# A graph network on one core: the fifth recurrent step computed with tokens on the partitions

## The chip, the cores and the metric

The kernel runs on one core of one Trainium2 chip. The metric is the device time of one execution in microseconds (us); three executions are shown by their median. A profiled execution adds a trace: every instruction with its engine, start, length and tiles. The engines are TensorE (PE: matrix products and transposes), VectorE (DVE), ScalarE (ACT), GpSimd (POOL) and SyncE (SP, which here issues nearly all transfers).

## The reference

128 graphs of 64 nodes, 256 features per node, in f32. Four layers follow each other, each as `x = x + layer(relu(layernorm(x)))`: two attention layers with the graph's adjacency (8 heads), five steps of a gated recurrent unit over the graph, and a gated graph convolution. The recurrent layer is what changes:

```
def _gru_cell(m, h, w_ih, w_hh, b_ih, b_hh):
    gi = m @ w_ih.T + b_ih
    gh = h @ w_hh.T + b_hh
    i_r, i_z, i_n = jnp.split(gi, 3, axis=-1)
    h_r, h_z, h_n = jnp.split(gh, 3, axis=-1)
    r = jax.nn.sigmoid(i_r + h_r)
    z = jax.nn.sigmoid(i_z + h_z)
    n = jnp.tanh(i_n + r * h_n)
    return (1.0 - z) * n + z * h
A = (adj != 0).astype(x.dtype)
h = x
for l in range(weight.shape[0]):            # 5 steps
    m = jnp.einsum('bnd,de->bne', h, weight[l])
    agg = jnp.einsum('bij,bid->bjd', A, m)
    h = _gru_cell(agg, h, w_ih, w_hh, b_ih, b_hh)
return h * mask[..., None]
```

## The kernel before

Two graphs make a pair (128 tokens, one per partition), four pairs a group of 512 tokens, and 16 groups make the input. A group passes through `front` (both attention layers), `entry` (the norm ahead of the recurrence), five steps of `gru`, and `back` (the last layer), while its neighbours are in other stages.

**The recurrent step.** `h` stands with features on the partitions: 128 partitions, two blocks of features, 512 tokens in two halves of 256. The step's matrix `weight[l]` is multiplied into `w_ih` beforehand (`fuse_weights`), so a step sums neighbours first (`agg`, small 64*64 tiles) and then needs the products of `h` with `w_hh` and of `agg` with the fused `gv`. Each 2x2 block product is done by Strassen's seven products in Winograd's form instead of eight: `product(i)`, i = 1 to 7, on blocks of `h` and `agg` and on differences of blocks (`Th`, made by POOL, and `Ta`, made by DVE). In each product the 128x128 weight block is the stationary operand and 256 tokens move, once for each of three gates and both inputs: 42 matmuls of 256 columns. They accumulate in four PSUM banks (`gb`, `gc` for the gates r and z, `nb`, `nc` for n), which all groups share through four slots of the tag `g`, taken in order. ACT copies partial sums out (`saved`), DVE adds a bank and a copy (`summed`), and `update` computes the gates: tanh on ACT, products on DVE, one subtraction on POOL. After steps one to four `turned` transposes the new `h` on TensorE (`hT`), because the next neighbour sum wants tokens on the partitions. The last group's fifth step is done by halves of tokens (`by_halves`, `update_half`), so that its first half can go on early.

**The last layer.** `back_half` turns the final `h` back to tokens on the partitions by eight TensorE transposes a group (`hx`, line 1375), adds it to `x` under the node mask (line 1382), takes the norm, and makes three products by seven (`l3b`, `l3c`; 384 columns) or, at the end, plainly (`f`, `gate`). `adjT`, the transposed adjacency of a group scaled by its degree, comes from `blk` (`adjblk`), which POOL fills from the adjacency tile in `front`.

**What sets the order.** Nothing runs in the order of the source. `Plan` collects every operation with a cost, an engine and a key (a due time in units of a group, set by `strand(base, span)` around the stage), and then picks for each engine, in time by its own costs, the ready operation that is due first. Banks and buffers are slots that it hands out. `CHANGE`, `BESIDE`, `ALONE` and `TURNING` are its costs and preferences for changes of TensorE's tile form (`WIDE`, 64*64, 64*32, transposes); `FRONT`, `BACK`, `STEP`, `LOCK`, `ENTRY`, `FIRST`, `FUSE` and their kin place the stages. The result is one fixed order of instructions for each engine.

Names in the trace: `gv`, `gates` fused weights and their copy in HBM; `qw`, `kept` the same for attention; `s`, `o` scores and weighted values of attention; `e` the exponentials; `xn`, `lnT`, `hT` the norm and its transposes; `cp` copies (`p1g`, `ug` and so on); `sg`, `sn` gates.

## Time and profile before

| | before |
|---|---|
| median of 3 executions | 2500.83 us (2500.80 to 2502.65) |
| the profiled execution, its own time | 2501.22 us |
| its span, first to last instruction | 2499.3 us |
| granted TensorE clock | 0.998 |
| DMA issues: fused weights `gv` | 80 of 1344 KB, 5.9 us to landing |
| DMA issues: `qw` | 203 of 192 KB, 2.4 us to landing |

The span is what the trace covers; the profiled time has 1.9 us around it. A busy share is an average over all stages, so the views in the prediction also take one stage alone. In a line of the timeline stand start and length in us, engine, source line, operation, output and inputs, sizes and count. In a line of the groups: busy us, mean ns of one, and what ended the idle time before it. In a line of the waits: total us, times, longest.

### The profile page before, as it was taken

How to read it: one execution, taken by the hardware profiler on the slowest of the kernel's cores; microseconds unless marked ns; L12 is line 12 of the kernel's file. 1: busy time of each engine (PE TensorE's matmuls, PEld its weight loads, DVE VectorE, ACT ScalarE, POOL GpSimd, SP SyncE). 2: the span in 40 equal slices, each digit the busy share in tenths (PEclk: the TensorE clock that was granted, in tenths of full speed). 3: DMA queues.
4: the chain of work that ended last, by engine and by line, in shares of the span. 5: the costliest groups of instructions: out<-in, count | busy, mean ns of one | idle time of the engine just before them, and what ended most of it. 6: DMA issues, size and time to landing. Idle time of an engine off the chain costs nothing.

```text
span 2499.3 us, 58765 instructions
## 1 busy us (share of the span) xinstructions
PE 2476.8 (99%) x24057; PEld 2130.1 (85%) x24057; DVE 1880.6 (75%) x4396; ACT 1308.5 (52%) x2654; POOL 895.9 (36%) x894
## 2 busy tenths in 40 slices
PE   9999999999999999999999999999999999999997
PEld 7788888888888888888888888888888888888885
DVE  6667777777777777787778777787777777877776
ACT  3455554555555455555555555555454555645544
POOL 5633433334233342433434233343333424332221
PEclk9999999999999999999999999999999999999999
DMA  6422212112222121212113122122211212211110
GB/s 211 158 71 86 72 54 98 65 53 84 72 80 72 61 75 66 100 52 80 59 63 102 50 97 74 53 80 72 80 68 60 76 66 80 68 50 71 52 69 19
DMA packets 78267, 188.60 MB, mean 75 GB/s; under 512 B 14803, under 2 KB 66853, under 8 KB 67109
## 3 DMA queue, kind: packets, MB, share of 16 engines
q1 hardware_dynamic: 77872, 184.71, 21.7%
q8 instruction: 192, 3.15, 0.5%
q14 instruction: 87, 0.70, 0.1%
q10 hardware_dynamic: 116, 0.04, 0.0%
HBM read 166.70 MB, written 18.02 MB: 74 GB/s over the span
## 4 chain that ended last, share of the span: by engine, by line
PE 97%; DVE 1%; ACT 0%; issue 0%; DMA 0%; POOL 0%; DVEq 0%; ACTq 0%
PE gb L994 22%; PE gc L994 17%; PE nb L994 11%; PE nc L994 8%; PE qkvb L711 6%; PE qkvc L711 5%; PE y L879 4%; PE agg L1034 3%; PE l3b L1339 3%; PE s L775 3%; PE l3c L1339 2%; PE hT L547 2%; PE lnT L547 2%; PE o L843 2%; PE o L851 1%; PE gv L930 1%
## 5 line engine op out<-in xcount | busy, mean ns | idle before, releaser
L1103 POOL TENSOR_TENSOR sn<-h,sn 128x512 f32<-128x512 f32 x158 | 202.9, 1287 | 544.5 <-ACT sn L1101 544.5
L533 POOL TENSOR_TENSOR rstd<-pw,few 128x2 f32<-128x2 f32 x128 | 96.3, 755 | 490.1 <-DVE pw L532 445.2
L994 PE MATMUL gb<-Th,w_hh 128*128 128x256 f32 x960 | 249.3, 382 | 0.0
L994 PE MATMUL gb<-Ta,gv 128*128 128x256 f32 x960 | 246.8, 380 | 0.0
L963 POOL TENSOR_TENSOR Th<-h 128x256 f32<-128x256 f32 x160 | 121.2, 778 | 299.8 <-PE nb L994 196.3
L799 POOL TENSOR_TENSOR e<-e,mask 128x512 f32<-128x512 f32 x128 | 177.5, 1406 | 111.5 <-ACT e L797 111.4
L994 PEld LDWEIGHTS gb<-Ta,gv 128*128 128x128 f32 x960 | 177.6, 190 | 22.1 <-issue 0.2
L994 PEld LDWEIGHTS gb<-Th,w_hh 128*128 128x128 f32 x960 | 175.6, 190 | 23.9 <-issue 2.4
L1101 ACT ACTIVATE sn<-sn,b_n 128x512 f32<-128x512 f32 x158 | 113.9, 722 | 143.8 <-DVE sn L1099 143.8
L1105 DVE SCALAR_TENSOR_TENSOR sn<-sg,sn 128x512 f32<-128x512 f32 x158 | 120.5, 769 | 74.4 <-POOL sn L1103 74.2
L994 PE MATMUL gc<-h,w_hh 128*128 128x256 f32 x640 | 167.7, 384 | 0.1
L994 PE MATMUL gc<-agg,gv 128*128 128x256 f32 x640 | 164.3, 379 | 0.0
L1086 ACT ACTIVATE sg<-sg,b_rz 128x512 f32<-128x512 f32 x158 | 106.5, 714 | 81.2 <-DVE sg L1066 81.2
L963 POOL TENSOR_TENSOR Th<-h,Th 128x256 f32<-128x256 f32 x160 | 144.8, 905 | 8.4 <-DVE h L1107 2.8
L552 ACT ACTIVATE hT<-lnT 128x512 f32<-128x512 f32 x96 | 57.1, 594 | 166.9 <-PE lnT L547 166.8
L994 PE MATMUL nb<-Ta,gv 128*128 128x256 f32 x480 | 144.0, 382 | 0.0
L994 PE MATMUL nb<-Th,w_hh 128*128 128x256 f32 x480 | 143.1, 380 | 0.0
L1097 DVE SCALAR_TENSOR_TENSOR sn<-sg,sn 128x512 f32<-128x512 f32 x158 | 117.7, 752 | 32.8 <-ACT sn L1208 28.3
L994 PEld LDWEIGHTS gc<-h,w_hh 128*128 128x128 f32 x640 | 116.2, 190 | 26.6 <-ACT sn L1208 4.0
L1099 DVE SCALAR_TENSOR_TENSOR sn<-sn 128x512 f32<-128x512 f32 x158 | 136.6, 871 | 2.4
L1047 DVE TENSOR_TENSOR Ta<-agg 128x256 f32<-128x256 f32 x160 | 100.2, 643 | 50.5 <-PE nb L994 27.7
L994 PEld LDWEIGHTS gc<-agg,gv 128*128 128x128 f32 x640 | 121.3, 190 | 16.7 <-issue 0.2
(228 smaller groups left out, 6559.4 us busy)
## 6 DMA issues: line engine op xcount, KB each, us to landing
gv<-gates SPq DMA_DIRECT2D x80, 1344.0 KB, 5.9
qw<-kept SPq DMA_DIRECT2D x203, 192.0 KB, 2.4
x<-in_x_dram SPq DMA_DIRECT2D x32, 256.0 KB, 2.9
out_dram<-x SPq DMA_DIRECT2D x32, 256.0 KB, 2.5
gates<-gv SPq DMA_DIRECT2D x5, 1344.0 KB, 5.7
adjq<-in_adj_dram SPq DMA_DIRECT2D x8, 256.0 KB, 4.7
gw<-in_L_gnn_weight_dram SPq DMA_DIRECT2D x5, 256.0 KB, 6.2
kept<-s SPq DMA_DIRECT2D x8, 128.0 KB, 1.9
```

The source lines that it names most:

```text
L711: nc.tensor.matmul(bk[:, j * P : (j + 1) * P], lhs, rhs, start=first and j == 0, stop=True, skip_group_check=True)
L799: pool(1225, lambda e=e: nc.gpsimd.tensor_tensor(e.tile, e.tile, bias_at(pp)[:, None, :].to_broadcast([P, 4, 2 * NODES]), op=ALU.mult), [e ...
L963: pool(690, lambda: nc.gpsimd.tensor_tensor(T[:, i, :], x(), y(), op=ALU.subtract), reads, [(T, i)])
L994: nc.tensor.matmul(bank_[:, col * HALF : (col + 1) * HALF], at(g, n), rhs(), start=first and j == 0, stop=True, skip_group_check=True)
L1047: vec2(dve(256), lambda: nc.vector.tensor_tensor(Ta[:, i, :], x(), y(), op=ALU.subtract), reads, [(Ta, i)])
L1086: sca(act(TOK, 1.5), lambda k=k, col=col: nc.scalar.activation(g_v[:, :, k, :], g_v[:, :, k, :], AF.Tanh, bias=b_rz[:, col : col + 1], sca ...
L1097: vec2(dve(TOK), lambda: nc.vector.scalar_tensor_tensor(a_(), r(), 1.0, a_(), op0=ALU.add, op1=ALU.mult), [*ts[0], n_v], [n_v])
L1099: vec2(dve(TOK), lambda: nc.vector.scalar_tensor_tensor(a_(), a_(), 0.5, b_(), op0=ALU.mult, op1=ALU.add), [n_v], [n_v])
L1101: sca(act(TOK, 1.5), lambda: nc.scalar.activation(a_(), a_(), AF.Tanh, bias=b_n[:, oc : oc + 1]), [n_v, b_n], [n_v])
L1103: pool(1230, lambda: nc.gpsimd.tensor_tensor(b_(), hh(), a_(), op=ALU.subtract), [*hp, n_v], [n_v])
L1105: vec2(dve(TOK), lambda: nc.vector.scalar_tensor_tensor(b_(), z(), 1.0, b_(), op0=ALU.add, op1=ALU.mult), [*ts[1], n_v], [n_v])
L1339: pe(mm(384), lambda: nc.tensor.matmul(bk[:, : 3 * P], b(), w3[:, :, n, :], start=first, stop=True, skip_group_check=True), [w3, *reads], ...
```

## The change

In the fifth step the operands change places: a block of 128 tokens of `h`, `agg` or their differences is the stationary operand, and the weights of all three gates move, 384 columns at once. The result has tokens on the partitions, so that the step works on `ht` (the transposed `h` that the neighbour sum used) and leaves its result there; `back_half` reads it, and `hx` goes. A bank now holds one half-block of 128 tokens with four parts: the n gate's input side, r, z, and the n gate's hidden side; `fuse_weights` stores the last step's gates in the order n, r, z for that. Biases lie along the free dimension, so they can no longer ride on ACT as a scalar per partition: they are rows (`b_row`, loaded by six DMAs and summed once by POOL), which POOL adds to each saved copy. The block of product 4, which has no saved copy to add, leaves its banks by four ACT copies (`taken`), and DVE adds the bias rows. The gates' tanh becomes one ACT instruction over 1024 elements. `adjT` is made in `back`, from a `blk` that two SP DMAs of 64 KB per group fill from HBM in place of POOL's copies. Buffer counts follow (`h` 4 to 3, `ht` 2 to 3, `adjT` 4 to 2), and the planner gets other costs and due times.

```diff
-CHANGE = ((0, 95, 95, 0), (190, 0, 170, 140), (150, 135, 30, 100), (0, 95, 95, 0))
-BESIDE = 0.45
-ALONE = 0.15
-TURNING = 0.25
+CHANGE = ((0, 95, 95, 0), (290, 0, 170, 190), (250, 135, 30, 150), (0, 95, 95, 0))
+BESIDE = 0.52
+ALONE = 0.17
+TURNING = 0.46
...
-FRONT_LAST = 0.05
-FRONT_SPAN = 0.95
-BACK = -0.1
-BACK_LAST = 0.3
+FRONT_LAST = 0.17
+FRONT_SPAN = 1.03
+BACK = 0.0
+BACK_LAST = 0.43
...
-STEP = 0.0
-STEP_LAST = -0.1
-STEP_SPAN = 0.5
-LOCK = 0.35
-BACK_END = 0.15
-ENTRY = -0.05
-FIRST = -1.2
-FIRST_SPAN = 1.0
+STEP = -0.08
+STEP_LAST = -0.07
+STEP_SPAN = 0.4
+LOCK = 0.23
+BACK_END = 0.18
+ENTRY = 0.63
+FIRST = -1.31
+FIRST_SPAN = 1.02
...
-FUSE = -1.1
-FUSE_SPAN = 0.2
+FUSE = -1.22
+FUSE_SPAN = 0.33
...
+        b_row = new("b_row", [P, 2, 4, P], 1)
...
+        dma(768, load_b, [], [b_row, more], 6)
+        pool(1225, lambda: nc.gpsimd.tensor_tensor(
+            b_row[:, :, 1:3, :], b_row[:, :, 1:3, :], more.tile, op=ALU.add), [b_row, more], [b_row])
...
+            if by_token:
+                tokens.send(ht)
+                final[g] = ht
+                yield
+                continue
...
+    def last_step(nm, h, Th, Ta, agg, gv, banks, operand, by_both, whole, halves):
+        def product(i, which, of_h, first=False):
+            n = WEIGHTS[i]
+            b, reads = operand(i, h, Th, by_both) if of_h else operand(i, agg, Ta, whole)
+            w = w_hh if of_h else gv
+            for t in range(2):
+                bk = banks[which][t]
+                pe(mm(384), lambda t=t, bk=bk: nc.tensor.matmul(
+                    bk[:, P:] if of_h else bk[:, : 3 * P], b()[:, t * P : (t + 1) * P], w[:, :, n, :],
+                    start=first, stop=True, skip_group_check=True), [w, reads], [bk])
...
+        def saved(which, n, oc):
+            out = []
+            for t in range(2):
+                c = new("cp", [P, 4, P], 5, f"{n}{t}_{nm}")
+                bk = banks[which][t]
+                sca(act(512), lambda c=c, bk=bk: nc.scalar.activation(
+                    c.tile, bk.tile.rearrange("p (g f) -> p g f", g=4), AF.Copy), [bk], [c])
+                pool(1225, lambda c=c: nc.gpsimd.tensor_tensor(c.tile, c.tile, b_row[:, oc], op=ALU.add),
+                     [c, b_row], [c])
+                out.append(c)
+            return out
...
+        def summed(oc, half, which, others):
+            sg, sn = s[half if halves else oc]
+            for t in range(2):
+                bk, p = banks[which][t], 2 * t + oc if halves else 2 * half + t
+                o, o_at = others[t], lambda o=others[t]: o.tile
+                for dst, key, part in ((sg, "g", lambda x: x[:, 1:3, :]), (sn, "n", lambda x: x[:, 0:4:3, :])):
+                    vec(dve(256), lambda dst=dst, part=part, bk=bk, p=p, o_at=o_at: nc.vector.tensor_tensor(
+                        dst[:, p], part(bk.tile.rearrange("p (g f) -> p g f", g=4)), part(o_at()), op=ALU.add),
+                        [bk, o], [(dst, p)])
...
+        def taken(oc, half, which):
+            ps = slice(oc, PAIRS, 2) if halves else slice(2 * half, 2 * half + 2)
+            for t in range(2):
+                bk, p = banks[which][t], 2 * t + oc if halves else 2 * half + t
+                for dst, part in zip(s[half if halves else oc], (slice(1, 3), slice(0, 4, 3))):
+                    sca(act(256), lambda dst=dst, part=part, bk=bk, p=p: nc.scalar.activation(
+                        dst[:, p], bk.tile.rearrange("p (g f) -> p g f", g=4)[:, part, :], AF.Copy), [bk], [(dst, p)])
+            for dst, part in zip(s[half if halves else oc], (slice(1, 3), slice(0, 4, 3))):
+                vec2(dve(512), lambda dst=dst, part=part: nc.vector.tensor_tensor(
...
+        summed(0, 0, 1, saved(0, "p1", 0))
...
+        both(5, 1, True)
+        p5 = saved(1, "p5", 1)
+        both(6, 0)
+        u = saved(0, "u", 0)
+        both(3, 1)
+        summed(0, 1, 1, u)
+        update(0)
+        both(7, 0)
+        summed(1, 1, 0, p5)
+        both(4, 0)
+        taken(1, 0, 0)
+        update(1)
+        yield
...
-        for gp in range(2):
-            s = slice(gp * NODES, (gp + 1) * NODES)
-            pool(350, lambda s=s: nc.gpsimd.tensor_copy(blk[s, :, s], adjq[s, sel, :]), [adjq], [(blk, gp)])
...
+        def fill():
+            for gp in range(2):
+                s = slice(gp * NODES, (gp + 1) * NODES)
+                nc.sync.dma_start(blk[s, :, s], adj_t[s, g * PAIRS : (g + 1) * PAIRS, :])
+
+        dma(128, fill, [], [blk], 2)
...
-        pe(437, turn, [(h, (0, half)), (h, (1, half)), ident], [ps], mode=TURN)
...
-                xt[:, p, :], ps[:, i * D : (i + 1) * D], cols[:, 18 + t : 19 + t], xt[:, p, :],
+                xt[:, p, :], h_by_token[:, p, :], cols[:, 18 + t : 19 + t], xt[:, p, :],
```

Removed with it are `by_halves` and `update_half`; the last group's fifth step takes another order of the same new products (6, 7, 4, then 5 and 3), by halves of tokens.

## Prediction

> **What bounds the kernel now.** I read the page's first and fourth parts, then busy time by stage, then TensorE's waits, then its timeline.

> ```profile
> span 2499.3 us, 58765 instructions
> PE 2476.8 (99%) x24057; PEld 2130.1 (85%) x24057; DVE 1880.6 (75%) x4396; ACT 1308.5 (52%) x2654; POOL 895.9 (36%) x894
> PE 97%; DVE 1%; ACT 0%; issue 0%; DMA 0%; POOL 0%; DVEq 0%; ACTq 0%
> ```
> ```profile
> 1177.78:1329.89 152.11, 152.11 (x1504) 131.81 (x1503) 117.45 (x277) 81.59 (x167) 54.69 (x54) 1.00 0.22 73
> ```
> ```profile
> PE f L1310 <- ACT hT L552: 2.2, 2, 1.1
> ...
> PE hx L1375 <- DVE h L1141: 1.4, 1, 1.4
> ```

> The chain that ended last is 97% TensorE. The second fence is one period (one group of four pairs) from the middle: length, then busy time of PE, weight loads, DVE, ACT, POOL. TensorE has no gap in it at all, at full clock. All its listed waits add up to about 10 us, in the first 130 us and the last 40. So time changes by what is issued on TensorE, unless another engine comes so late that gaps open.

> A matmul's listed duration is modelled and overlaps the next, so I price by start to start:

> ```profile
> 1205.30 1.03 PE L994 MATMUL gb<-Th,w_hh 128*128 128x256 f32 x4
> 1206.16 0.60 PE L547 MATMUL hT<-ident,h 128*128 128x128 f32 x4
> 1206.60 0.60 PE L994 MATMUL nb<-h,w_hh 128*128 128x256 f32 x2
> ...
> 1209.19 0.59 PE L994 MATMUL nb<-Ta,gv 128*128 128x256 f32 x2
> 1209.72 1.10 PE L775 MATMUL s<-kexp,qk 64*64 64x128 f32 x32
> 1210.64 1.11 PE L1034 MATMUL agg<-A,ht 64*64 64x64 f32 x64
> 1211.68 0.66 PE L1280 MATMUL adjT<-ident,adjblk 128*128 128x128 f32 x4
> 1212.18 1.03 PE L994 MATMUL gb<-h,w_hh 128*128 128x256 f32 x4
> ```
> ```profile
> 123.86 1.10 PE L775 MATMUL s<-kexp,qk 64*64 64x128 f32 x32
> 124.90 1.13 PE L994 MATMUL gb<-Th,w_hh 128*128 128x256 f32 x4
> 125.86 0.61 PE L711 MATMUL qkvb<-hT,qw 128*128 128x128 f32 x4
> ```
> ```profile
> 2441.82 0.81 PE L1339 MATMUL l3c<-w,hTT 128*128 128x384 f32 x2
> 2442.47 0.81 PE L1339 MATMUL l3b<-w,hTT 128*128 128x384 f32 x2
> ```

> Each f32 matmul is two records. 1205.30 to 1206.16: four records of 256 columns take 0.86, so 0.216 each. 1206.16 to 1206.60: a transpose takes 0.109. 2441.82 to 2442.47: 384 columns take about 0.323 each. Small-tile work (s, o, agg: 64*64 or 64*32) costs at its edges. Entering: two records before s take 0.53 instead of 0.43, so 0.10. Ending: s takes 1.04 before a wide matmul (123.86 to 124.90) but 0.92 before agg of the same tile, so 0.12. After it: the first wide matmul costs 0.10 more (0.96 for four), a transpose only 0.06 more (0.50 for four).

> [...] L1099, from SBUF alone, averages 871 ns where POOL works beside it, and its twin L1132 689 ns in the tail, where POOL is nearly idle.

> **The change, part by part.**

> 1. *The turn back goes.* The fifth step leaves h by token, so hx (L1375) disappears:

> ```profile
> L1375 PE MATMUL hx<-ident,h 128*128 128x128 f32 x128 | 19.2, 274 | 1.4 <-DVE h L1141 1.4
> ```
> 128 x 0.109 = **-14.0 us**, all on the saturated engine.

> 2. *The fifth step's products.* Per group 42 matmuls of 256 columns become 28 of 384: the same 10,752 columns. 1344 records x 0.216 = 290.3 become 896 x 0.3225 = 289.0 to 289.4: **-0.9 us**. Weight loads fall by a third and stay hidden.

> 3. *Other durations in the plan.* They reorder only. I counted both built orders on PE. Of 208 small blocks (agg, s, o), those that follow one of the same tile go from 24 to 39; runs of small blocks from 138 to 152; runs left to a wide matmul from 118 to 93, to a transpose from 20 to 59. So +14 x 0.10 - 25 x 0.10 + 39 x 0.06 - 15 x 0.12 = **-0.6 us**.

> 4. *Other engines.* Durations from:

> ```profile
> L730 DVE TENSOR_TENSOR qk<-qkvc,qu 128x256 f32<-128x256 f32 x58 | 24.4, 420 | 32.5 <-PE qkvc L711 30.4 <-ACT qu L726 0.6
> L1103 POOL TENSOR_TENSOR sn<-h,sn 128x512 f32<-128x512 f32 x158 | 202.9, 1287 | 544.5 <-ACT sn L1101 544.5
> L1058 ACT ACTIVATE p1g<-gb 128x512 f32<-128x512 f32 x80 | 47.7, 597 | 45.0 <-PE gb L994 44.9
> ```
> DVE: three pairs of sums (686 + 743 ns) become 12 sums of 420 and two bias adds of about 685: 4.3 to 6.4, +2.1 us a group, 34 in all: 77% of the new span. POOL: 96 bias adds x 1.29 = 124, less 19 for the block copies (L1265): 40%. ACT: about 0.7 less a group, since two gates share one tanh of 1024 (an estimate of 1.03 us, from 597 at 512 and 376 at 256, L724). None comes near 99%, so I cost these at **nothing in the middle**; the cover is TensorE's other work. That cover is what the rivals test.

> 5. *Moved to SP.* 32 fills of adjblk (64 KB) and six bias loads join 411 DMAs. A fill waits only for the adjT transposes of a group one period earlier; behind it stand gate-weight loads (5.9 us to land), needed a step later. The bias loads stand behind the kept stores; behind them stand the second gates store and w3. The bias rows are first needed in step five of group 0, over 200 us later. POOL's one extra add is 1.3 us there. Nothing on the path; bounds 0 to +3 for the start.

> 6. *The tail.* Here other engines set the end. From product 4's end to the last group's first lnT, TensorE had 12.5 us of work and the chain took 14.2 (2456.9 to 2471.12). The new order leaves 11.4 us. The new chain is four copies 1.5, two adds 1.4, tanh 1.0 and 0.6, five DVE steps 3.4, x 0.85, norm 2.5: 11.3, and over a dozen handovers and sums of the other half squeezed in, some 14 again. So it is about 2.6 late instead of 1.7: **+0.9**; bounds -2 (the hx wait of 1.4 goes and nothing replaces it) to +5 (the b_row adds queue behind the other half on DVE).

> Sum: -14.0 - 0.9 - 0.6 + 0.9 = **-14.6 us** against the profiled 2501.2 (span 2499.3 and 1.9 around it), so 2486.6. The median shown, 2500.8, is 0.4 lower: 2486.2, rounded to **2486**. Without parts 5 and 6, a period should fall from 152.0 to about 151.0.

> **Rivals.** A change under 0.2%, 5.0 us, is about what a measurement of this kernel cannot tell from none.

> *A, likeliest (0.70):* as summed; own range 2481 to 2491.

> *B, gaps close too (0.11):* of 10 us of waits at start and end up to half go, since the reordered start and the turnless tail suit the engines. 2476 to 2481. For it: hx itself waited 1.4. Against: f after hT (2.2) is the same code.

> *C, start and last groups open gaps (0.12):* the spread-out weight fusion, or the DVE-bound last chain at its upper bound, costs 5 to 15: 2491 to 2501, about half of it still faster. For it: these are the only places with waits now.

> *D, slower (0.07):* DVE becomes late inside every fifth step. Product 5 restarts bank gc only when product 2 has been summed out; in the new order 1.96 us of other PE work stands between, the two sums of a bank need 0.84, and p1 must already have gone ACT 0.6, POOL 1.29. In the list, the bias adds share POOL with mask products (1.4 each) and the next Th. If the sums come 2.1 us late, the gain of 0.98 a period is gone; 3.5 us late adds 1.4 x 16 = 22: 2508. [...] Against: product 1's copies stand 9 us ahead of product 5, and in the old order the same bank had 1.74 us for one sum of 0.69 and no wait shows.

> That the plan's new durations do not help is counted in part 3; were they worth nothing, 2486.8.

> **How the numbers follow.** A and B are faster; of C about half lies below 2495.8, the rest within 0.2%; D is slower. Faster 0.87, same 0.06, slower 0.07. Range 2478 to 2496: it leaves out D, B's lower half and C's end.

> **What would show it.** Right: hx gone; 896 records of 384 columns at 0.323 in the step; a middle period of 151.0 with PE busy throughout; PE waits in all still near 10 us. Wrong: a wait of gc or nc on DVE in every period (D), a period above 151.5, or waits before 130 us and after 2400 us that exceed 15 us (C).

## The result, and the profile after

| | median (us) | lowest to highest | ratio to the kernel before, 95% interval |
|---|---|---|---|
| changed kernel | 2510.56 (8 runs) | 2507.73 to 2512.51 | 1.0033 [1.0024, 1.0042] |
| before, beside it | 2502.66 (8 runs) | 2500.80 to 2503.07 | |
| changed kernel, a second session | 2505.95 (14 runs) | 2502.09 to 2509.91 | 1.0016 [1.0008, 1.0024] |
| before, beside it | 2501.19 (32 runs) | 2500.43 to 2503.16 | |

The change made the kernel slower, by 4.8 to 7.9 us, where a gain of some 15 was forecast. The changed kernel also spreads more: 8 us between its own runs where the kernel before has 3. The spread, and the part of the loss that falls in the middle, have one cause, found below (experiments 1 to 5); the start and the tail lose time of their own.

The page of the kernel after, its first and fourth parts:

```profile
span 2508.4 us, 58053 instructions
PE 2475.2 (99%) x23481; PEld 2027.1 (81%) x23481; DVE 1928.9 (77%) x4524; ACT 1290.7 (51%) x2634; POOL 992.0 (40%) x959
```
```profile
PE 90%; DVE 8%; issue 1%; ACT 1%; POOL 0%; DMA 0%; DVEq 0%; ACTq 0%
```

DVE has its forecast 77%, POOL its 40%: the busy shares were right and gave no warning. The chain tells more: TensorE fell from 97% of it to 90%, DVE rose from 1% to 8%.

Two periods of the middle (from one group's `adjT` transposes to the next), busy time by stage of the kernel after: length, then PE, weight loads, DVE, ACT, POOL.

```profile
711.09:862.28 151.19, 151.19 (x1473) 125.12 (x1466) 118.98 (x285) 80.41 (x166) 60.38 (x58) 1.00 0.22 73
1014.34:1166.38 152.04, 151.63 (x1472) 125.02 (x1466) 120.42 (x285) 80.41 (x166) 59.80 (x58) 1.00 0.22 73
```

The work and its order are the same in both. One is 151.2 long without a gap, near the 151.0 forecast; the other is 152.0, and TensorE has lost 0.4 us to idle and more to records that start late. The forecast period exists, but not always.

TensorE's waits of the kernel after (total us, times, longest):

```profile
PE hom L1482 <- DVE F L1402: 5.4, 1, 5.4
PE qkvb L726 <- DVE v L747: 4.6, 11, 1.5
PE y L894 <- issue: 1.6, 1, 1.6
...
PE hT L562 <- DVE h L1130: 1.3, 2, 1.0
```

`hx` is gone from the list. New are one wait of 5.4 us in the tail and one on DVE's line 747 that comes back eleven times, nine of them in the middle (2.8 us together).

**An account of the span.** I took the interval from each TensorE record's start to the next and subtracted the median of such intervals (same kind, columns and neighbours) in the trace of before. The sum of these prices is the issue sum; what is above it is the excess: gaps and records at a lower rate. The start is the first 450 us, the tail the last 95 us before TensorE's last record. The span adds 1.35 us ahead of the first record and 11 to 13 after the last.

| kernel | issue sum | excess, start | middle | tail | span of the profiled run |
|---|---|---|---|---|---|
| before | 2466.1 | 8.0 | 3.5 | 7.7 | 2499.3 |
| changed | 2450.5 | 16.0 | 14.9 | 14.2 | 2508.4 |
| changed, second session | 2450.5 | 17.2 | 10.8 | 13.8 | 2504.9 |
| no_bias | 2450.5 | 14.4 | 4.9 | 13.9 | 2496.7 |
| new_plan | 2466.7 | 12.0 | 4.6 | 12.2 | 2509.3 |
| old_plan | 2461.5 | 10.9 | 20.6 | 20.3 | 2526.1 |
| swap | 2450.5 | 14.5 | 6.9 | 14.6 | 2499.4 |
| swap_mm | 2455.7 | 14.8 | 6.3 | 8.1 | 2497.7 |

The forecast saving of issue came in full: 2466.1 - 2450.5 = 15.6. It was eaten by 8.0 us more excess in the start, 11.4 in the middle and 6.5 in the tail; the stretch after the last record gave 1.3 back. Sum +9.0; the spans differ by 9.1.

### The profile page after: what moved, and what is told of

Same layout as the page of the kernel before. It is cut to its first block, busy times and chain, and to the rows that moved or that the text cites. A ratio compares the mean times of both kernels' runs of the same rounds, so it can differ in the third digit from the quotient of the medians.

```text
span 2508.4 us, 58053 instructions
## 1 busy us (share of the span) xinstructions
PE 2475.2 (99%) x23481; PEld 2027.1 (81%) x23481; DVE 1928.9 (77%) x4524; ACT 1290.7 (51%) x2634; POOL 992.0 (40%) x959
## 4 chain that ended last, share of the span: by engine, by line
PE 90%; DVE 8%; issue 1%; ACT 1%; POOL 0%; DMA 0%; DVEq 0%; ACTq 0%
PE gb L1012 17%; PE gc L1012 13%; PE nb L1012 9%; PE nc L1012 6%; PE qkvb L726 5%; PE y L894 5%; PE qkvc L726 4%; PE agg L1057 3%; PE l3b L1424 3%; PE gb L1194 3%; PE nb L1194 3%; PE s L790 2%; PE lnT L562 2%; PE l3c L1424 2%; PE hT L562 2%; PE o L858 2%
## 5 line engine op out<-in xcount | busy, mean ns | idle before, releaser
L1126 POOL TENSOR_TENSOR sn<-h,sn 128x512 f32<-128x512 f32 x128 | 165.0, 1289 | 670.6 <-ACT sn L1124 670.5
L1012 PE MATMUL gb<-Th,w_hh 128*128 128x256 f32 x768 | 197.6, 380 | 0.9 <-DVE sg L1089 0.9
L1012 PE MATMUL gb<-Ta,gv 128*128 128x256 f32 x768 | 197.3, 379 | 0.0
L1012 PEld LDWEIGHTS gb<-Ta,gv 128*128 128x128 f32 x768 | 141.5, 190 | 19.8
L894 PE MATMUL y<-w_L_gnn_Wo,oT 128*128 128x256 f32 x512 | 142.8, 383 | 2.0 <-issue 1.6
L1128 DVE SCALAR_TENSOR_TENSOR sn<-sg,sn 128x512 f32<-128x512 f32 x128 | 105.9, 827 | 48.3 <-POOL sn L1126 48.3
L726 PEld LDWEIGHTS qkvb<-hTQ,qw 128*128 128x128 f32 x696 | 101.5, 191 | 31.3 <-DVE v L747 11.4
L894 PEld LDWEIGHTS y<-w_L_gnn_Wo,oT 128*128 128x128 f32 x512 | 95.3, 190 | 30.0 <-issue 4.4
L803 POOL TENSOR_TENSOR x<-x,r_L_gnn_bo 128x512 f32<-128x512 f32 x64 | 83.1, 1299 | 85.7 <-DVE xn L592 74.6
L726 PE MATMUL qkvb<-hTQ,qw 128*128 128x128 f32 x696 | 108.4, 278 | 4.7 <-DVE v L747 4.6
```

The costliest lines, as they stand in the source:

```text
L726: nc.tensor.matmul(bk[:, j * P : (j + 1) * P], lhs, rhs, start=first and j == 0, stop=True, skip_group_check=True)
L894: pe(mm(256), lambda i=i, c=c: nc.tensor.matmul(py[:, i * D : (i + 1) * D], oT[:, i, c, :], w_o[:, c, :], start=c == 0, stop=c == 1), [(oT ...
L1012: nc.tensor.matmul(bank_[:, col * HALF : (col + 1) * HALF], at(g, n), rhs(), start=first and j == 0, stop=True, skip_group_check=True)
L1126: pool(1230, lambda: nc.gpsimd.tensor_tensor(b_(), hh(), a_(), op=ALU.subtract), [*hp, n_v], [n_v])
L1128: vec2(dve(TOK), lambda: nc.vector.scalar_tensor_tensor(b_(), z(), 1.0, b_(), op0=ALU.add, op1=ALU.mult), [*ts[1], n_v], [n_v])
```

## The experiments

Theory L: POOL's new bias adds stretch the DVE instructions that run beside them (line 1128: 0.69 us in the median, up to 1.80), DVE comes late and TensorE waits. Rivals: P, the plan's new due times do it; W, DVE has no room for more work, stretched or not; T, the new products themselves.

**1. The adds left out (no_bias).**

```diff
-pool(1225, lambda c=c: nc.gpsimd.tensor_tensor(c.tile, c.tile, b_row[:, oc], op=ALU.add),
+pool(1225, lambda c=c: None,
```

> The changed kernel with the order of all instructions kept, but POOL's six bias adds per group on the saved copies (line 1209) left out; so the biases of three of the four blocks of the fifth step are missing from the output. Theory L [...]: the adds come in back-to-back pairs of nearly 6 us, stretch DVE beside them (0.69 to 1.8 us an instruction), and DVE's lateness opens about 1 us of TensorE gaps per period. Then the middle period falls from 152.04 to about 151.1 and the time to 2499 to 2503, a little below the kernel before. Rival P (plan): the new due times, not the adds, make DVE late: period 152.0, time 2509 to 2511. Rival T (TensorE): the 384-column products themselves cost more than I priced, or hold up later ones: no change either.

Measured: 2498.41 us, ratio 0.9985 [0.9977, 0.9993]; spread 4 us. Every middle period is 151.0, the middle's excess 4.9. So the adds make the middle's loss; P and T fall there. How they make it, by stretching DVE's instructions or by coming late themselves, this run can't tell. Start and tail stay as they were.

**2. The plan's numbers alone, both ways (old_plan, new_plan).** Only the constants at the top of the file are exchanged, from `CHANGE` to `FUSE_SPAN`.

> The new fifth step and back stage with the planner's costs and due times of the kernel before. By counting its built order of TensorE, at the prices of the trace of before, the issue sum is 2461.5 us (before 2466.1, after 2450.5); before's span is 33 us above its sum, after's 58. Theory L (the adds of the new step make the gaps of the middle, whatever the plan): 10 us of gaps in the middle and some in the tail remain, so 2461.5 + 33 + 10 to 17 + 2 = 2507 to 2514. Rival P (the plan makes all the gaps): 2461.5 + 33 + 2 = 2497. Start (first 450 us): L says nothing of it; if the lost 8 us there come from the due times of the weight fusion, they are absent here.

> The kernel before with the planner's new costs and due times only. Issue sum of its built order 2466.7. Theory L: no middle gaps, since there are no adds: 2466.7 + 33 + 2 = 2502, up to 2510 if the start's 8 us come from the new due times. Rival P: 2466.7 + 58 + 2 = 2527.

Measured: old_plan 2528.22 us, ratio 1.0106 [1.009, 1.0121]; new_plan 2510.41, ratio 1.0035 [1.0023, 1.0047]. old_plan is above all that was expected of either; new_plan is just above the upper end of L and far below P. The table shows why. In new_plan, without any bias add, the middle is clean (4.6), but start and tail have 4.0 and 4.5 more than before: the due times alone can make half of the start's loss and most of the tail's. In old_plan the new step fits its surroundings worse: 11 us more issue, and in the middle TensorE waits for ACT's copies of `agg` (line 1063; 6.4 us in five waits).

So the step and its due times belong together; neither alone has the middle of the pair.

**3. The adds on DVE (dve_bias, dve_kept).** The add becomes `nc.vector.tensor_tensor`. In dve_bias the planner builds a new order around it, in dve_kept the instruction goes out where POOL's would have, and TensorE's order is that of the changed kernel.

> The six bias adds per group on DVE (512 elements, 0.69 us) in place of POOL; the planner rebuilds the order, with an issue sum of 2452.9 (2450.5 before this edit). DVE gets 4.1 us a group, 66 in all, and loses the stretch. Theory L [...]: the middle gaps go as without the adds, whose span was 46.2 above its sum: 2452.9 + 46.2 + 1.8 = 2501. Rival W (it is DVE's mere work that is late): DVE is busier than before this edit, the gaps grow: 2512 or more.

> All six bias adds a group on DVE instead of POOL as before, but put in at the places that the planner gave POOL's adds, so that the order of TensorE stays that of the changed kernel (issue sum 2450.5). The earlier run with a rebuilt order had many small gaps in all periods. If that order was the cause: 2498 to 2502. If DVE has no room for 4.1 us more a group (rival W): 2508 to 2514.

Measured: dve_bias 2512.16, ratio 1.0041 [1.0028, 1.0055]; dve_kept 2507.87, ratio 1.0022 [1.0014, 1.0029]. What L expected failed both times, and W's numbers were met or missed by 0.1 us, so W has a part in it. Without POOL's adds, in the kept order, every full period is at least 151.5 long, and DVE is late again:

```profile
PE qkvc L726 <- DVE v L747: 4.4, 12, 0.7
```

DVE is 77% busy over the whole run, and yet 4.1 us more a group do not fit without a delay.

**4. Two of the six adds gone (p5_kept).** The copies of product 5 go without bias, and `taken` adds it to all four pairs instead of two:

```diff
-dst[:, ps], dst[:, ps], b_row[:, oc, part, :][:, None].to_broadcast([P, 2, 2, P]), op=ALU.add),
+dst[:, at], dst[:, at], b_row[:, oc, part, :][:, None].to_broadcast([P, k, 2, P]), op=ALU.add),
```

> The changed kernel, order kept, with the two POOL bias adds on the copies of product 5 gone; their bias comes with the two DVE adds that the block of product 4 needs anyway (line 1232), widened from 512 to 1024 elements, so by about 0.5 us each. The run of four POOL adds back to back (5.8 us beside DVE) becomes one of two. Theory L: DVE's lateness halves and falls below what makes TensorE wait; the gaps of 1 us a period go, as without any adds: 2498 to 2501, and the spread between runs shrinks from 8 us to about 4. Rival W (any more work on DVE opens gaps): 2505 or more.

Measured: 2508.75, ratio 1.0027 [1.0016, 1.0037]. L's time, 2498 to 2501, was missed. The waits on line 747 in the middle are gone, as L said, but no period is shorter than 151.5: with the widened adds, `lnT` waits some 0.30 us for `xn` in each. The spread fell to 4 us. One small loss was traded for another.

**5. What makes the two kinds of period.** In one trace (the changed kernel, second session) I laid a short period and a long one side by side. Timeline, the stretch around the first bias add of product 5: start, length, engine, line. First the short one:

```profile
1048.07 1.27 POOL L1126 TENSOR_TENSOR sn<-h,sn 128x512 f32<-128x512 f32 x1 [5.05 <-ACT sn L1124]
...
1049.39 3.24 POOL L1209 TENSOR_TENSOR p<-p,b_row 128x512 f32<-128x512 f32 x2
1049.40 0.68 DVE L1128 SCALAR_TENSOR_TENSOR sn<-sg,sn 128x512 f32<-128x512 f32 x1
...
1051.01 0.48 DVE L1503 SCALAR_TENSOR_TENSOR o<-o,F 128x256 f32<-128x256 f32 x1
```
Then the long one:
```profile
1199.11 1.27 POOL L1126 TENSOR_TENSOR sn<-h,sn 128x512 f32<-128x512 f32 x1 [5.04 <-ACT sn L1124]
...
1200.43 2.95 POOL L1209 TENSOR_TENSOR p<-p,b_row 128x512 f32<-128x512 f32 x2
1200.45 1.80 DVE L1128 SCALAR_TENSOR_TENSOR sn<-sg,sn 128x512 f32<-128x512 f32 x1
...
1202.51 1.16 DVE L1503 SCALAR_TENSOR_TENSOR o<-o,F 128x256 f32<-128x256 f32 x1
...
1203.92 0.38 PE L726 MATMUL qkvb<-hTQ,qw 128*128 128x128 f32 x1 [0.31 <-DVE v L747]
```

POOL's line 1126 ends and releases DVE's line 1128; at that same moment ACT's copy has released the bias add on POOL. Where DVE starts 10 ns after POOL, it takes 0.68 us and POOL's two adds take longer (3.24). Where it starts 20 ns after, DVE takes 1.80 and POOL's take 2.95. Then `v` (line 747) is late, and TensorE waits. Laid record by record, TensorE loses 0.6 us before that `qkvb`, 0.2 before the next `hT` (line 562, which waits for DVE's `h` of line 1130) and 0.2 right after it, so 1.0 in all. I read all 78 such meetings in the six traces with this order there: DVE at most 20 ns behind, 0.68 us (37 times); 20 ns or more, 1.74 to 1.80 us (41 times). The changed kernel had 11 of 13 on the slow side in the trace of its first session, 6 in that of its second.

Theory R: which of the two starts first decides the kind of period. Two experiments push one side by a memset of 64 columns on a small tile of its own.

```diff
 def add_bias(c, t, n, oc):                     # pool_last
+    if n == "p5" and not t:
+        nc.gpsimd.memset(idle.tile, 0.0)
     nc.gpsimd.tensor_tensor(c.tile, c.tile, b_row[:, oc], op=ALU.add)
 def turn(b_=b_, z=z):                          # dve_last
+    nc.vector.memset(idle.tile, 0.0)
     nc.vector.scalar_tensor_tensor(b_(), z(), 1.0, b_(), op0=ALU.add, op1=ALU.mult)
```

> The changed kernel, order kept, with one POOL memset of 64 columns (some 0.15 us) put ahead of the first bias add of product 5. In the trace of the changed kernel, a period is 151.0 long where DVE's line 1128 (released by POOL's line 1126 at the same moment as the add by ACT's copy) starts within 10 ns of the add and takes 0.68 us, and 152.1 where it starts 20 ns after it and takes 1.80. Theory R [...]: the memset lets DVE start first in every period; all periods are 151.0 to 151.1, the middle loses 4 us instead of up to 13, and the time is 2499 to 2502 with half the spread. If DVE is late for another reason: 2503 to 2510, both kinds of period as before.

> The opposite: a DVE memset of 64 columns (under 0.15 us) ahead of every line 1128, eight a group, nothing on POOL. Theory R: POOL always starts first, every period is 152.1 or a little more: 2509 to 2513, small spread. If the race doesn't matter: 2503 to 2510, both kinds of period.

Measured: dve_last 2511.22 (2508.08 to 2512.66), ratio 1.0035 [1.0023, 1.0047]: every period 152.1, as expected (its memset took 0.11 us). pool_last 2513.14, ratio 1.0042 [1.0028, 1.0055]: the opposite of what I expected, every period 152.1. Its timeline (line numbers are moved by two and more: 1130 is 1128, 1506 is 1499, 1207 is 1209) explains it:

```profile
1049.13 0.95 DVE L1506 TENSOR_SCALAR F<-o 128x256 f32<-128x256 f32 x1
1049.78 0.15 POOL L1206 MEMSET idle<- 128x64 f32 x1
1049.89 3.00 POOL L1207 TENSOR_TENSOR p<-p,b_row 128x512 f32<-128x512 f32 x2
1050.00 1.75 DVE L1130 SCALAR_TENSOR_TENSOR sn<-sg,sn 128x512 f32<-128x512 f32 x1
```

DVE's instruction ahead of the race took 0.95 us instead of 0.86 and so DVE came 0.11 us behind POOL again. Only the slow side had been forced so far, so for the other side serve POOL's two adds of product 5 in the opposite order: the first then waits for the later copy.

```diff
-pool(1225, lambda c=c: nc.gpsimd.tensor_tensor(c.tile, c.tile, b_row[:, oc], op=ALU.add),
+pool(1225, lambda c=c, t=t: add_bias(out, t, n, oc),
+# with
+def add_bias(out, t, n, oc):
+    for c in () if n == "p5" and not t else out[::-1] if n == "p5" else out[t : t + 1]:
+        nc.gpsimd.tensor_tensor(c.tile, c.tile, b_row[:, oc], op=ALU.add)
```

> The changed kernel, order of TensorE kept, with POOL's two bias adds of product 5 in the opposite order: first the one whose ACT copy ends about 0.7 us later. Nothing is added or left out. POOL then starts its pair 0.7 us after DVE's line 1128 has started instead of within 20 ns of it. Theory R: line 1128 takes 0.68 us in every period, all middle periods are 151.0 to 151.2, the excess over the issue sum grows by 4 us through the middle instead of 4 to 14, and the time is 2498 to 2502. If the pair stretches DVE as much where it now lies (lines 1503, 1505), the period is 151.6 to 152.1 and the time 2507 to 2512.

Timeline of swap, and one of its periods:

```profile
1044.81 0.68 DVE L1128 SCALAR_TENSOR_TENSOR sn<-sg,sn 128x512 f32<-128x512 f32 x1
1045.49 2.67 POOL L1204 TENSOR_TENSOR p<-p,b_row 128x512 f32<-128x512 f32 x2 [0.75 <-ACT p L1211]
```
```profile
1060.25:1211.33 151.08, 151.08 (x1468) 125.30 (x1467) 119.02 (x287) 80.42 (x166) 59.81 (x57) 1.00 0.23 75
```

Measured: 2502.80 us (2501.36 to 2506.69), ratio 1.0008 [0.9999, 1.0016]. DVE takes 0.68, POOL's pair starts when it is done, all full periods of the middle are 151.0 to 151.4, and TensorE has no gap in the one shown. The time is 0.8 us above the range expected. With the same instructions in the same number, the median is 3 us below the changed kernel's second session and 8 below its first; by the ratios to the kernel before, each run beside its own, it is 2 and 6 us, and the intervals of swap and of the second session overlap. The evidence is in the periods: dve_last makes all of them long, swap all of them short. So the race is shown from both sides.

**6. The tail.** Timeline of the kernel after:

```profile
2472.99 0.61 PE L1482 MATMUL hom<-F,adjT 128*128 128x256 f32 x2
2479.04 1.22 PE L1482 MATMUL hom<-F,adjT 128*128 128x256 f32 x2 [5.43 <-DVE F L1402]
...
2481.80 2.07 PE L1395 MATMUL f<-w,hT 128*128 128x256 f32 x4 [0.69 <-ACT hT L567]
```

After an idle stretch of 5.4 us, four records of `f` take 1.86 (the next instruction starts at 2483.66) instead of 0.86. TensorE works at half rate for some 7 us, up to 2485.91, where the granted clock, at 0.50 from 2475.67 on, goes back to 1.00.

First, less work for DVE (tail_off): `tensor_copy` of `f` to ACT, the gate's bias of group 14 to POOL.

```diff
-vec(dve(256), lambda ...: nc.vector.tensor_copy(F[i][:, 0, :], pf[:, :D]), ...
+sca(act(256), lambda ...: nc.scalar.activation(F[i][:, 0, :], pf[:, :D], AF.Copy), ...
-if g + 1 == n_groups:        # bias of the gate on POOL
+if g + 2 >= n_groups:
```

> The changed kernel with two pieces of DVE's work in the tail moved: the copies of f in the plain products (line 1402) go to ACT, and the bias adds of group 14's gate (line 1478) to POOL. This takes five DVE instructions of 0.42 us out of the stretch from 2464 to 2479 us, in which DVE has no gap and TensorE waits. Theory DVE-tail: the next lnT comes about 2 us sooner and the end 1.5 to 2.5 us, against the changed kernel beside it; the wait of 5.4 us for line 1402 goes, or turns into a wait of lnT for xn. Rival (the tail hangs on the chain of handovers, not on DVE's load): within 0.5 us.

Measured: 2507.86, ratio 1.0025 [1.0016, 1.0034], not faster than the changed kernel beside it (2505.95); the wait moved to the next instruction and grew: `lnT` (line 562) waits once for `xn` of DVE (line 592), 8.5 us. What `lnT` needs is the end of a long chain over DVE; the copies were only in its neighbourhood. Nor do the old due times of the last groups (lasts_old: five constants from before) mend it:

> The changed kernel with the due times of the last groups (FRONT_LAST, BACK_LAST, STEP_LAST, LOCK, BACK_END) from before; issue sum 2450.7. If these made the tail's 5.5 us: 2500 to 2502. If the new last step's own chain on DVE makes it: 2505 to 2507; and if they suit it worse, more.

Measured: 2505.80, ratio 1.0019 [1.001, 1.0029], as expected if the step's own chain makes the tail; tail excess 15.3.

Second, is it the idle stretch that halves the rate? Spare work is put in front of the waiting `hom`, into an unused half of its bank; the result is not used.

```diff
 def weigh(p=p, f=f, ph=ph):
     if g + 2 == n_groups and p == 1:
+        for _ in range(46):   # awake46; 28 in awake
+            nc.tensor.transpose(ph[:, D : D + P], ident.tile, ident.tile)
+        for _ in range(12):   # pool_last_mm and swap_mm, instead
+            nc.tensor.matmul(ph[:, D:], ident.tile, w3[:, 0, 0:2, :], start=True, stop=True)
     nc.tensor.matmul(ph[:, :D], adjT[:, p, :], f(), start=True, stop=True)
```

> The changed kernel with 28 spare transposes of the identity (about 3 us) on TensorE inside the 5.4 us idle stretch of the tail, ahead of the last neighbour product of group 14, into an unused part of its bank. After that stretch the records ran at half rate for some 6 us. If the idle stretch lowered the clock, the records after it run at full rate and the end comes 1.5 to 3 us sooner: 2507.5 to 2509. If the tail hangs on DVE's chain alone, or the rate fell for another reason, within 0.5 us of the changed kernel.

> As the kernel with 28 spare transposes, but 46 (5.0 us), so that about 0.6 us of idle is left ahead of the last neighbour product of group 14. With 28, 2.4 us were left and the records after it still ran at half rate; in all traces so far, records after gaps of up to 1.8 us ran at full rate and those after 1.9 us or more at half rate for 3 to 7 us. If that is the cause, no half-rate stretch follows here, and the end comes 1.5 to 3 us sooner than in the changed kernel beside it. Otherwise within 0.5 us.

> The kernel with POOL's memset, and twelve spare matmuls of 256 columns (5.2 us) in the idle stretch of the tail in place of the 46 transposes tried before, which did not prevent the half-rate records. If matmuls count as work where transposes don't, the records after run at full rate and the end comes 2 to 3 us sooner than without them; if the rate falls anyway, within 0.5 us.

With 28 and with 46 transposes a half-rate stretch still followed. Of awake46, then of pool_last_mm (its line 1402 is `f` too):

```profile
2468.57 5.18 PE L1485 MATMUL hom<-ident 128*128 128x128 f32 x46
2476.80 2.08 PE L1395 MATMUL f<-w,hT 128*128 128x256 f32 x4 [1.05 <-ACT hT L567]
```
```profile
2476.07 5.34 PE L1492 MATMUL hom<-w,ident 128*128 128x256 f32 x24
...
2484.30 1.13 PE L1402 MATMUL f<-w,hT 128*128 128x256 f32 x4 [1.06 <-ACT hT L569]
```

```profile
2469.86:2473.27 3.41, 3.41 (x34) 3.41 (x33) 3.41 (x11) 0.84 (x2) 0.00 (x0) 1.00 0.00 0
2473.27:2476.68 3.41, 1.96 (x11) 0.99 (x9) 3.41 (x12) 1.25 (x4) 0.82 (x1) 1.00 0.23 77
```
```profile
2482.46:2485.88 3.42, 2.35 (x10) 1.66 (x11) 3.42 (x11) 1.63 (x5) 0.00 (x0) 1.00 0.04 15
```

The first window holds nothing but spare transposes, and after it the clock stays at 1.00. It is 0.50 only after the second, in which TensorE was busy for 1.96 us. In pool_last_mm the same waits lie differently to the window's edges, TensorE is busy for 2.35 us, and the clock stays at 1.00. The waits lie differently to the edges from run to run, and there are two traces with transposes and two with matmuls. So it is not shown that matmuls keep the rate where transposes don't; where the window fell is a rival that no run here separates.

From the last `adjT` to TensorE's last record there are 69.4 us in pool_last and 67.8 in pool_last_mm, whose median was 2511.22, ratio 1.0035 [1.0021, 1.0049]; that is 1.9 less than pool_last's, where 2 to 3 were expected, and the intervals overlap. The times of awake (2503.66, ratio 1.0004 [0.9996, 1.0012]) and awake46 (2504.04, ratio 1.0006 [0.9998, 1.0014]) are lower than the changed kernel's in its first session. One reason is fewer long periods: 4 and 8 of 13 slow meetings in their traces, against 11. To see that, the changed kernel was run again:

> The changed kernel as it is, on the same chip as the three beside it. Its periods are of two kinds in the traces (some with the 1 us gap beside the bias adds, some without), and the kernel with 28 spare transposes, same order, had fewer of them and 2503.7 us. If the share of such periods differs from session to session, this run lands between 2503 and 2511; if 28 transposes in the tail brought the 7 us, it stays at 2510 to 2511.

Measured: 2505.95 us, the second session of the first table, with 6 slow meetings. The share of them differs from session to session and from run to run. That does not explain awake46, which ran in the same session and had 8 of them in its trace, and whose median is still 1.9 us lower. In its tail the clock is halved for 3.41 us, in the changed kernel's for 6.83, so its transposes may have gained something; the intervals overlap, and the question stays open.

**7. The start (start_old).** `FIRST`, `FIRST_SPAN`, `FUSE`, `FUSE_SPAN` from before.

> The changed kernel with the due times of the first stage and of the weight fusion (FIRST, FIRST_SPAN, FUSE, FUSE_SPAN) from before; issue sum 2452.3, 1.9 more. If these due times made the start's extra 6.5 us of gaps, the excess up to the second group's adjT falls from 14 to 17 us to some 9, and the time to 2501 to 2503. If the new step's loads and fills did: it stays, 2507 to 2508.

Measured: 2519.98, ratio 1.0072 [1.0058, 1.0085]. The start's excess fell only to 13.0, and the constants reach further than their names: the whole order changed with them, the middle has 19.2 us of excess and the tail 18.1. This test settled little.

**8. The best of them (swap_mm).** Swapped adds and twelve spare matmuls together.

> As swap, and with the twelve spare matmuls in the idle stretch of the tail, after which no record ran at half rate, where 46 transposes had not prevented it; the last TensorE record then came 1.6 us sooner after the last adjT. Expected: 1.5 to 2 us less than swap, 2496.5 to 2500, that is below the kernel before (2501.5) and the changed one.

Measured: 2501.14 us (2499.21 to 2502.59), ratio 0.9997 [0.9989, 1.0006]; 1.7 us below swap in the medians, as expected, but 1.1 above the expected range, and the tail from the last `adjT` is 67.8 instead of 69.7. It is as fast as the kernel before and not measurably faster. With the middle repaired, what remains between it and the forecast is the start (+6.8 us over before) and the tail's chain.

## Why the prediction was wrong

**Parts 1 to 3, what TensorE issues: right as a sum.** The `hx` line is gone, and in the tail's timeline two records of `gc` (line 1194, 384 columns) start 0.65 us apart, 2464.75 to 2465.40. The 0.3225 of part 2 stands in the trace of before as well: of 236 intervals from one record of 384 columns to the next (line 1339), 153 are 322 or 323 ns. Predicted -15.5, counted -15.6. But "were they worth nothing, 2486.8" was wrong: part 3 counted due times and step jointly. With the old numbers, the new step would have issued 11 us more (2461.5).

**Part 4, "nothing in the middle": the step that failed first.** It measured +11.4 us in the first session and +7.3 in the second. The cover named, "TensorE's other work", covers DVE's lateness only while TensorE's fixed order has something else to do, and the work behind `v` and `h` had none. I priced 96 adds by their length (1.29 us; 1.40 to 1.48 measured) and looked at shares, 77% and 40%, which came out exactly. What an add does to the instruction beside it was the price that mattered: 1.1 us more for line 1128, in those meetings where POOL gets ahead. The trace of before had shown such a price: I quoted 871 ns for line 1099 beside POOL and 689 alone, as an average, but its shortest, median and longest are

```profile
L1099 DVE SCALAR_TENSOR_TENSOR sn<-sn x158: 643/691/1769, 123.0 to 2435.2; 128x512 f32<-128x512 f32 x158
```

so most of them lost nothing and some lost 1.1 us, and the average is not a price for any one instruction.

**The rivals.** C said that start and last groups would open 5 to 15 us of gaps; they opened 14.5, but I gave it 0.12 and the middle nothing. D had the engine and the price right (a DVE a few us late in each fifth step takes the gain) and the place wrong: the sums into `gc` that it watched were in time; late were `v` of the next attention stage and `h` of another group's step, which stand behind line 1128 on DVE. Its chance of 0.07 was too low for a step that puts 96 POOL adds beside a DVE at 75%.

**Part 5, the start: 0 to +3, measured +8.0.** SP's queue shows in none of the start's waits. new_plan has 4.0 of the 8.0 without any part of the new step, so the new costs and due times alone can make half; which of them is not shown, since start_old, with four of them put back, still has 13.0. Of the start's waits for another engine, those for DVE lead (line 747, 1.8 us, and line 1130, 1.3). A pause of `y` (1.6 us in the list above) has no releaser in the trace, with records at half rate after it in nine of 15 traces. A packet of instructions is fetched in the same 10 us, beside a 1344 KB load of `gv`; that they belong together was not tried, and the rest of the start stays open.

**Part 6, the tail: +0.9, bounds -2 to +5; measured +6.5, less 1.3 after the last record.** TensorE had the 11.4 us of work that I counted after product 4 (2461.96 to 2473.4). The chain, taken at "some 14", took 18.1 (to `lnT` at 2480.05): on DVE, without a gap from 2464 on, the other half's sums and the end of group 14 stand between its links. That opened the idle stretch of 5.4 us, and half-rate records after it added some 1.6 to 1.9 us more (what the tails of pool_last_mm and swap_mm are shorter by), which no part of the sum had. So the size of this term failed too: its chain was taken 4 us too short.

## What to carry to other kernels

A busy share tells what fits on average, not what meets: where two engines can hold each other up (here 1.80 us instead of 0.68 for the same DVE instruction), look for the instruction that starts beside the new one, and price how much longer that one takes, not only the new one's length. When a fixed order makes two engines start within some tens of nanoseconds of each other (here 20 ns divided the two kinds), measure over many periods and many runs, and let one of them wait for a later event on purpose. A wait is only worth removing if nothing else on the same chain ends with it: the copies of `f` ended last in the list, `xn` was right behind.

## What the runs showed of the hardware

- Line 1128 on DVE (128x512, f32) took 0.68 us where it started before POOL's bias add or up to 20 ns behind it, and 1.74 to 1.80 us where it came 20 ns or more behind; so it was in all 78 meetings. POOL's two adds took 3.24 us in the one case and 2.95 in the other (a period of each in the changed kernel, second session). The start times in the profile don't give the order to the last 20 ns, and what the two engines share there is not shown.
- In awake46 a window of 3.41 us with nothing but transposes left the clock at 1.00; it was 0.50 after the next, with 1.96 us of work. With twelve spare matmuls in a stretch of waiting no half-rate stretch followed in two traces, and their tails were 1.6 and 1.9 us shorter. Whether transposes and matmuls differ in this is not shown.
- The rate was lost after shorter pauses than the tail's 5.4 us. In the start of 15 traces stands one pause of TensorE at the same place, between two records of `y` (taken from start to start, less the price of a record). After pauses of 1.80 to 1.82 us (five traces) the next records ran at full rate, after 1.89 to 2.44 us (eight) six to nine of them at half rate; at 1.87 us there is one trace of each. The windows of 3.41 us tell these two apart: in p5_kept the pause lies within one window and the clock fell, in swap it lies across two and the clock stayed. In the window with most of the pause TensorE was busy for 1.40 to 1.70 us where the clock fell and for 1.75 us or more where it stayed. This split holds for the start alone: in the tail of no_bias the clock stayed after a window with 1.43, in that of awake46 it fell after one with 1.96. Half rate for eight records costs some 1.7 us (8 x 0.216), about as much as the pause itself.
